# A two-layer image kernel: its last slots and last convolution as one written list, and the convolution's kernel from a stored fixed part

## The chip, the core and the metric

The kernel runs on one core of a Trainium2 chip. The metric is the device time of one execution in microseconds. Before the change the median of 3 runs is 1951.01 us (1948.79 to 1951.85).

## What is computed

Four images of 128 channels and 128x128 pixels go through two layers, each added to its input. Layer 0 works on pixels (tokens) of 128 channels; layer 1 is a 3x3 convolution with a gate per channel. `_gn` normalises groups of 4 channels over the whole image. Cut to what matters:

```python
def _block(t):                       # t: tokens x 128 channels
    t = _ln(t, ln0); y1 = _ln(t, ln1)
    t = t + silu(y1) @ W_out.T
    y2 = _ln(t, ln2); wht = y2 @ W_whiten.T
    k = square(relu(wht @ W_key.T))
    return t + sigmoid(wht @ W_recep.T) * (k @ W_value.T)
def _conv(x):                        # its weight is that of expert 0
    avg = x.mean(axis=(2, 3))
    se = sigmoid(relu(avg @ se_w1.T) @ se_w2.T)
    return (conv3x3(x, weight[0], padding=1) + bias[0]) * se[:, :, None, None]
x = x + _block(_gn(x)) + _block(_gn(x).transpose(0, 1, 3, 2)).transpose(0, 1, 3, 2)
x = x + _conv(_gn(x))
```

The two calls of `_block` see the same tokens in another order, so their sum is computed once and doubled.

## The kernel before, in words

**Layer 0** takes a pair of chunks of 512 pixels (a group g of `PAIR`) at a time: 16 groups an image, 64 in all. A group goes through some 40 named operations: `u` (normalise, ACT), `Tu` (turn, PE), `bn` (statistics, DVE), `nb` (norm terms, nine or six small operations on POOL, `norm_terms`), `t`, `g`, `b` (ACT, POOL, POOL), `z`, `Tz`, `silu`, `att`, `T`, then the third norm's terms, which are turned (`Tr`), copied (`rc`), stored to HBM (`W`, rd) and read back over all partitions (`R`), `cp` (y2), eight keys `pk`, their relu and square `re`, `sq` on ACT, eight values `kv`, the gate `pr`, `th`, `q`, and the sum into x (`S`, `x` on POOL), with the statistics `bx` for layer 1. The digits after a name are the half of the pair and the part.

**Layer 1** is a convolution on blocks of 16 rows (8 an image), computed in groups of four output rows by six transformed inputs: `p`, `q`, `p2`, `q2` and `v0` to `v5` on DVE, six products `c0` to `c5` on PE (three pairs of matmul passes each, `product`, lines 536 to 538), `e1`, `e3` on ACT, and `a`, `b`, `c`, `d`, `y0` to `y3`, `ca`, `d8` on DVE. The finished block is stored with one DMA of 1 MB (line 633). Each product takes one bank of PSUM; while layer 0 runs, all six share the one bank of tag `conv`.

**The order.** `ORDER` is written by hand: one slot runs each of its 114 operations with the group or block that is due (`u1:0` is for group s of slot s, `x11:3` for group s - 3). Inside `tc.manual_schedule()` each engine runs its instructions in the order written. The first 20 slots have an order of their own (`FIRST`). Slots go on to 68, so the last ones have ever fewer operations. The convolution of batch 3 stands behind the slots, outside the manual schedule, block after block.

**conv_setup(b)** (lines 253 to 330) makes the convolution's kernel of one image. It needs the statistics of the whole image: `mv` (line 226), `pm` (a matmul with `gmat`), mg, d, q, `pv`, ve, rs on POOL (line 240), avg, `p1`, a1, `p2`, the tanh `se` on ACT, `dg`, `pg`, `row`. Then cw, the 128x1152 weight, is scaled by rs and row (line 289), ident is added to its middle tap, and six transformed kernels uw0 to uw5 are formed from it (lines 305 to 328) on ACT and DVE. It is a generator: a slot gives it a step after every fifth operation, and what is left runs at the slot's end. It starts in the slot after the image's last group is done. The matmuls of the chain take banks of the tag `h`, which the keys use too (two banks). `input_norm(b)` is a similar, shorter chain for layer 0's input.

In the tables, PEld is the weight load, SP the queue that issues the DMAs.

Of the kernel before, what the change touches and what calls it, by code (L numbers as in the profile page):

```python
# [9 lines left out]
F32 = mybir.dt.float32  # L10
# [35 lines left out]
FIRST_SLOTS = 20  # L46
PAUSE = 2

SQUARES = ("AAAA", "AAAA")
FIRST_SQUARES = ("DAAA", "DAAA")  # L50

ON_GPSIMD = set()
ODD = {"v5a", "v5b", "c4", "c", "d", "y1", "y2", "ca", "d8", "c0", "y0", "c5", "y3"}
EVEN = {
    "p", "q", "v1", "v2", "p2", "q2", "c1", "e1", "c2", "a", "b", "v3", "v4", "c3", "e3",
# [5 lines left out]
def conv_preact_kernel(  # L61
# [63 lines left out]
    def bank(tag, name, bufs=2):  # L125
        return ps.tile([P, CH], F32, tag=tag, name=name, bufs=bufs)
# [93 lines left out]
    def col(name):  # L220
        return stat.tile([P, 1], F32, tag=name, name=name)
# [25 lines left out]
    def input_norm(b):  # L247
# [2 lines left out]
        nc.vector.scalar_tensor_tensor(nb, mg, -1.0, rs, ALU.mult, ALU.mult)  # L250
        gn0[b] = rs, nb

    def conv_setup(b):

        cw = wg.tile([P, 9, P], F32, tag="ring", name="cw", bufs=1)
        nc.sync.dma_start(cw, conv_w)
        d, mg, rs = yield from group_norm(st1.pop(b), "1")
        avg = col("avg")  # L260
        nc.vector.tensor_tensor(avg, d, rs, ALU.mult)
        mg6 = col("mg6")
        nc.vector.tensor_scalar(mg6, mg, 6.0, None, ALU.mult)
        yield
        p1 = bank("h", "p1")
        nc.tensor.matmul(p1[:NSE, 0:1], s1, avg, start=True, stop=True)
        yield
        a1 = stat.tile([NSE, 1], F32, tag="a1", name="a1")
        nc.vector.tensor_scalar(a1, p1[:NSE, 0:1], 0.0, None, ALU.max)
        yield  # L270
        p2 = bank("h", "p2")
        nc.tensor.matmul(p2[:, 0:1], s2, a1, start=True, stop=True)
        yield
        se = col("se")
        nc.scalar.activation(se, p2[:, 0:1], AF.Tanh, scale=0.5)
        yield
        nc.vector.tensor_scalar(se, se, 1.0, 0.5, ALU.add, ALU.mult)
        beta = col("beta")
        nc.vector.scalar_tensor_tensor(beta, se, cb, mg, ALU.mult, ALU.add)
        dg = wk.tile([P, P], F32, tag="u", name="dg")  # L280
        nc.vector.tensor_scalar(dg, ident, se, None, ALU.mult)
        yield
        pg = bank("h", "pg")
        nc.tensor.matmul(pg[:, :P], mean_of, dg, start=True, stop=True)
        yield
        row = wk.tile([P, P], F32, tag="u", name="row")
        nc.scalar.mul(row, pg[:, :P], float(C))
        yield
        nc.vector.scalar_tensor_tensor(
            cw, cw, rs, row.rearrange("p (o c) -> p o c", o=1).to_broadcast([P, 9, P]),  # L290
            ALU.mult, ALU.mult,
        )
        nc.vector.tensor_tensor(cw[:, 4], cw[:, 4], ident, ALU.add)
        yield
        w0, w1, w2 = (cw[:, 3 * a : 3 * a + 3].rearrange("p b c -> p (b c)") for a in range(3))
        uw, u = {}, {}

        def form(i, freed):
            while b > 0 and freed and (freed, b * NBLK - 1) not in multiplied:
                yield  # L300
            uw[i] = wg.tile([P, 3, P], F32, tag="uw", name=f"uw{i}", bufs=9)
            u[i] = uw[i].rearrange("p b c -> p (b c)")

        w6 = wk.tile([P, 3 * P], F32, tag="z", name="w6", bufs=2)
        nc.scalar.mul(w6, w1, 1.0 / 6)
        tmp = wk.tile([P, 3 * P], F32, tag="u", name="tmp")
        nc.vector.tensor_tensor(tmp, w0, w2, ALU.add)
        yield
        for i in (1, 2):
            yield from form(i, None)  # L310
        nc.vector.scalar_tensor_tensor(u[1], tmp, -1.0 / 6, w6, ALU.mult, ALU.subtract)
        nc.vector.scalar_tensor_tensor(u[2], tmp, -1.0 / 6, w6, ALU.mult, ALU.add)
        yield
        w4 = wk.tile([P, 3 * P], F32, tag="z", name="w4", bufs=2)
        nc.scalar.mul(w4, w0, 0.25)
        nc.scalar.mul(w6, w6, 0.5)
        nc.vector.tensor_tensor(tmp, w4, w2, ALU.add)
        yield
        yield from form(3, None)
        yield from form(4, 1)  # L320
        nc.vector.scalar_tensor_tensor(u[3], tmp, 1.0 / 6, w6, ALU.mult, ALU.add)
        nc.vector.scalar_tensor_tensor(u[4], tmp, 1.0 / 6, w6, ALU.mult, ALU.subtract)
        yield
        yield from form(0, 2)
        nc.scalar.copy(u[0], w4)
        yield
        yield from form(5, 3)
        nc.scalar.copy(u[5], w2)
        gn1[b] = mg, mg6, beta
        uws[b] = uw  # L330


    S = {}
# [196 lines left out]
    def wide(tag, name):  # L530
        return wg.tile([P, Q, W], F32, tag=tag, name=name)

    def product(i, k, v, tag="conv", bufs=1):
        pc = bank(tag, f"m{i}", bufs).rearrange("p (q w) -> p q w", w=W)
        u = uws[k // NBLK][i]
        nc.tensor.matmul(pc, u[:, 1], v, start=True, stop=False)  # L536
        nc.tensor.matmul(pc[:, :, 1:W], u[:, 0], v[:, :, 0 : W - 1], start=False, stop=False)  # L537
        nc.tensor.matmul(pc[:, :, 0 : W - 1], u[:, 2], v[:, :, 1:W], start=False, stop=True)  # L538
        return pc

    def conv_op(op, k, tag="conv", bufs=1):
        mg, mg6, beta = gn1[k // NBLK]
        first, last = k % NBLK == 0, k % NBLK == NBLK - 1
        d1, d2, d3, d4 = (rows(k, s) for s in range(4))
        eng = nc.gpsimd if op in ON_GPSIMD else nc.vector

        def put(name, tag):
            S[name, k] = t = wide(tag, name)
            return t

        def get(name):
# [8 lines left out]
        elif op == "q":  # L560
            stt(put("q", "vt"), d1, -4.0, d3)
        elif op == "v1":
            stt(put("v1", "v"), get("p"), mg6, get("q"), ALU.add)
        elif op == "v2":
            eng.tensor_tensor(put("v2", "v"), get("p"), get("q"), ALU.subtract)
        elif op == "p2":
# [7 lines left out]
        elif op == "v0a":  # L574
            v0 = put("v0", "v")
            eng.tensor_tensor(v0[:, 1:Q], d4[:, 0 : Q - 1], d2[:, 1:Q], ALU.subtract)
            if first:
                nc.vector.tensor_scalar(v0[:, 0:1], d2[:, 0:1], -1.0, mg, ALU.mult, ALU.add)
            else:
                eng.tensor_tensor(  # L580
                    v0[:, 0:1], S.pop(("edge", k - 1)), d2[:, 0:1], ALU.subtract
                )
        elif op == "v0b":
            stt(get("v0"), get("v0"), 4.0, get("p2"))
        elif op == "v5a":
            v5 = put("v5", "v")
            eng.tensor_tensor(v5[:, 0 : Q - 1], d1[:, 1:Q], d3[:, 0 : Q - 1], ALU.subtract)
            if last:
                nc.vector.tensor_scalar(
                    v5[:, Q - 1 : Q], d3[:, Q - 1 : Q], -1.0, mg, ALU.mult, ALU.add  # L590
                )
            else:
                eng.tensor_tensor(
                    v5[:, Q - 1 : Q], rows(k + 1, 0)[:, 0:1], d3[:, Q - 1 : Q], ALU.subtract
                )
                S["edge", k] = wg.tile([P, 1, W], F32, tag="edge", name="edge", bufs=2)
                eng.tensor_copy(S["edge", k], d4[:, Q - 1 : Q])
# [3 lines left out]
        elif op[0] == "c" and len(op) == 2 and op != "ca":  # L601
            i = int(op[1])
            multiplied.add((i, k))
            S["m", i, k] = product(i, k, S.pop((f"v{i}", k)), tag, bufs)
        elif op == "e1":
            nc.scalar.activation(put("e1", "yt"), S.pop(("m", 1, k)), AF.Identity, bias=beta)  # L606
        elif op == "e3":
            nc.scalar.copy(put("e3", "yt"), S.pop(("m", 3, k)))
        elif op == "a":
# [37 lines left out]
    def in_stats(g, h, src):  # L647
        b, p = g // NP, g % NP
        if b not in st0:
            st0[b] = stat.tile([P, NCH, 6], F32, tag="st0", name=f"st0_{b}")  # L650
        nc.vector.bn_stats(st0[b][:, p * PAIR + h, :], src)  # L651

    def layer0_op(op, g):
# [32 lines left out]


    def parsed(text):
        return [(w.split(":")[0], int(w.split(":")[1])) for w in text.split()]

    order, first = parsed(ORDER), parsed(FIRST)
    depth = max(k for op, k in order if op not in EVEN and op not in ODD)
# [26 lines left out]
    def slot(s, order, repeated):  # L719
# [12 lines left out]
        for n, (op, k) in enumerate(order):  # L732
            g = s - k
            if op in EVEN or op in ODD:
                c = g - NP - LAG
                if 0 <= c < (B - 1) * NP and (c % 2 == 1) == (op in ODD):
                    conv_op(op, c // 2)
            elif op in ("in0", "in1"):
                h = int(op[2])
                for i in now[:1]:  # L740
                    in_stats(i, h, S["in", i][:, ts(h, CH)])
            elif 0 <= g < B * NP and (op, g) not in issued:
                issued.add((op, g))
                layer0_op(op, g)
            if n % 5 == 4:
                for chain in chains:
                    next(chain, None)
        for chain in chains:
# [7 lines left out]
    with tc.manual_schedule():  # L756
        for s in range(FIRST_SLOTS):
            slot(s, first, False)
        phase["first"] = False
        for s in range(FIRST_SLOTS - PAUSE, slots):  # L760
            slot(s, order, s < FIRST_SLOTS)


    for k in range((B - 1) * NBLK, B * NBLK):
        for op in (
            "p q v1 v2 p2 q2 c1 e1 v3 v4 c2 a b v0a v0b c3 e3 v5a v5b c4 c d y1 y2 ca d8 "
            "c0 y0 c5 y3"
        ).split():
            conv_op(op, k, "h" if op in ("c1", "c3", "c0") else "tr", 2)


# [40 lines left out]
```

## Time and profile before

| what | value |
|---|---|
| median of 3 runs | 1951.01 us |
| the profiled execution, whole | 1947.18 us |
| its span in the profile | 1945.4 us |
| PE busy | 1825.0 us (94%) |
| DVE busy | 1351.5 us (69%) |
| ACT busy | 1278.1 us (66%) |
| POOL busy | 1147.5 us (59%) |
| granted TensorE clock, mean | 0.99 |
| DMA, mean | 67 GB/s |

The profile is one execution. Matmuls are pipelined and their ends are modelled, so a PE that is shown busy need not be at its peak; the distances between the starts of matmuls are firm. A wait is put down to the instruction that came last. "issue" is time in which the engine waited for nothing that the profile shows. PEclk is the granted share of the full TensorE clock. A row of a group or of the timeline gives start, duration, engine, line, operation, output<-inputs and shapes, and in brackets the idle time before it with who ended it.

### The profile page before, as it was taken

The numbers are of one execution on the slowest core, as the hardware profiler recorded it, in microseconds if no ns is written. First come the engines' busy times: TensorE is split into PE (matmuls) and PEld (weight loads), VectorE is DVE, ScalarE is ACT, GpSimd is POOL, SyncE is SP. The second block draws the span as 40 slices with busy tenths as digits, with TensorE's granted clock in tenths as the row PEclk, the third lists the DMA queues.
The fourth block names the chain that finished last, engine by engine and source line by source line (L and its number), as shares of the span: only waits on it lengthen the run. The fifth ranks groups of instructions, "written<-read, shape, count | busy, mean of one in ns | idle before, by whom it ended". The sixth has DMA issues, their size and how long they took to land.

```text
span 1945.4 us, 21642 instructions
## 1 busy us (share of the span) xinstructions
PE 1825.0 (94%) x6154; PEld 944.2 (49%) x6154; DVE 1351.5 (69%) x3309; ACT 1278.1 (66%) x2493; POOL 1147.5 (59%) x1939
## 2 busy tenths in 40 slices
PE   2399999999999999999999999999999999997998
PEld 1355555554545554554455455455455555543343
DVE  5466676665777776776677777667677666764997
ACT  0688998877677767676777677676676777752100
POOL 0877888774666766666766666666666667630000
PEclk9899999999999999999999999999999999999999
DMA  5211111120222221122232122112101111110111
GB/s 206 61 55 55 55 55 55 65 67 22 76 87 82 82 98 65 44 67 78 76 98 90 56 73 77 66 55 77 48 35 60 66 66 55 44 44 34 44 76 76
DMA packets 38567, 130.72 MB, mean 67 GB/s; under 512 B 5408, under 2 KB 7088, under 8 KB 30256
## 3 DMA queue, kind: packets, MB, share of 16 engines
q1 hardware_dynamic: 36160, 128.47, 19.1%
q10 hardware_dynamic: 2288, 0.87, 0.2%
q8 instruction: 49, 0.80, 0.2%
q14 instruction: 70, 0.57, 0.1%
HBM read 95.50 MB, written 33.82 MB: 66 GB/s over the span
## 4 chain that ended last, share of the span: by engine, by line
PE 75%; POOL 9%; DVE 6%; ACT 4%; issue 3%; DMA 2%; ACTq 0%; POOLq 0%; DVEq 0%
PE pk L471 19%; PE kv L498 18%; PE m L536 8%; PE m L537 8%; PE m L538 7%; PE pr L489 4%; PE att L433 4%; POOL rs L397 3%; DVE st L380 2%; PE tt L349 2%; PE ut L349 2%; ACT t L356 2%; PE z1t L349 2%; DVE st L651 1%; POOL rs L396 1%
## 5 line engine op out<-in xcount | busy, mean ns | idle before, releaser
L471 PE MATMUL pk<-y,wk_s 128*128 128x512 f32 x1024 | 503.0, 599 | 8.6 <-DVE h L485 4.4
L498 PE MATMUL kv<-h,wv 128*128 128x512 f32 x1024 | 483.7, 595 | 0.0
L475 ACT ACTIVATE h<-pk,kbias 128x512 f32<-128x512 f32 x512 | 350.9, 686 | 152.0 <-PE pk L471 150.6
L397 POOL TENSOR_TENSOR rs<-rs,nhalf 128x8 f32<-128x8 f32 x192 | 317.6, 1654 | 15.1
L498 PEld LDWEIGHTS kv<-h,wv 128*128 128x128 f32 x1024 | 187.8, 191 | 215.4 <-issue 185.1
L356 ACT ACTIVATE t<-ut,nb,rs 128x128 f32<-128x128 f32 x512 | 192.5, 464 | 146.7 <-POOL nb L403 146.7
L481 ACT ACTIVATE h<-h 128x512 f32<-128x512 f32 x479 | 282.8, 630 | 4.5
L471 PEld LDWEIGHTS pk<-y,wk_s 128*128 128x128 f32 x1024 | 182.9, 191 | 209.0 <-issue 149.9
L518 POOL TENSOR_TENSOR x<-x,r 128x512 f32<-128x512 f32 x128 | 163.5, 1277 | 185.5 <-DVE r L514 185.5
L380 DVE BATCH_NORM_STATS2 st<-t 128x6 f32<-128x128 f32 x1024 | 219.1, 276 | 22.5 <-POOL t L416 20.1
L356 ACT ACTIVATE z<-t,nb,rs 128x128 f32<-128x128 f32 x512 | 210.3, 488 | 21.9 <-POOL nb L403 21.9
L536 PE MATMUL m<-v,uw 128*128 128x512 f32 x384 | 201.6, 607 | 16.1 <-ACT e L606 6.5
L412 POOL TENSOR_TENSOR t<-t,g 128x512 f32<-128x512 f32 x128 | 162.9, 1280 | 73.3 <-ACT t L356 73.3
L537 PE MATMUL m<-v,uw 128*128 128x508 f32 x384 | 196.4, 593 | 0.0
L538 PE MATMUL m<-v,uw 128*128 128x508 f32 x384 | 195.6, 591 | 0.0
L392 POOL TENSOR_TENSOR rs<-st 128x8 f32<-128x8 f32 x192 | 56.5, 294 | 223.4 <-DVE st L380 207.9
L416 POOL TENSOR_TENSOR t<-t,b 128x512 f32<-128x512 f32 x128 | 162.4, 1275 | 6.9
L493 ACT ACTIVATE r<-pr,rbias 128x512 f32<-128x512 f32 x128 | 87.6, 684 | 90.2 <-PE pr L489 84.6
L433 PEld LDWEIGHTS att<-wo,y 128*128 128x128 f32 x1024 | 128.2, 193 | 21.6 <-issue 13.8
L433 PE MATMUL att<-wo,y 128*128 128x128 f32 x1024 | 136.8, 277 | 1.9 <-ACT y L427 1.5
L380 DVE BATCH_NORM_STATS2 st<-ut 128x6 f32<-128x128 f32 x512 | 111.6, 284 | 37.7 <-PE ut L349 37.7
L489 PE MATMUL pr<-y,wr_s 128*128 128x512 f32 x256 | 132.0, 597 | 5.0 <-ACT h L475 4.7
(125 smaller groups left out, 2427.7 us busy)
## 6 DMA issues: line engine op xcount, KB each, us to landing
x<-in_x SPq DMA_DIRECT2D x32, 1024.0 KB
R<-rd SPq DMA_DIRECT2D x128, 256.0 KB
out<-x SPq DMA_DIRECT2D x32, 1024.0 KB
xs<-in_x SPq DMA_DIRECT2D x48, 512.0 KB
cw<-in_conv_w SPq DMA_DIRECT2D x4, 576.0 KB
rd<-rrow SPq DMA_DIRECT2D x64, 4.0 KB
wv<-in_w_value_t ACTq DMA_DIRECT2D x1, 256.0 KB
wkt<-in_w_key_t ACTq DMA_DIRECT2D x1, 256.0 KB
```

The lines of the kernel that those rows point to most:

```text
L356: nc.scalar.activation(dst[:, s, :], src[:, s, :], AF.Identity, bias=nb[:, i : i + 1], scale=rs[:, i : i + 1],)
L380: nc.vector.bn_stats(st[:, h * SUB + s, :], src[:, s, :])
L397: gp.tensor_tensor(rs, rs, nhalf, ALU.pow)
L433: nc.tensor.matmul(att[:, ts(s, P)], y[:, ts(s, P)], wo, start=True, stop=True)
L471: nc.tensor.matmul(pk, wk_s[:, ts(j, P)], S["y2", g, h], start=True, stop=True)
L475: nc.scalar.activation(k, S["pk", g, h, j], AF.Relu, bias=kbias[:, j : j + 1])
L481: nc.scalar.activation(k, k, AF.Square)
L489: nc.tensor.matmul(pr, wr_s, S["y2", g, h], start=True, stop=True)
L498: nc.tensor.matmul(S["kv", g, h], wv[:, j, :], S.pop(("h", g, h, j)), start=(j == 0), stop=(j == NH - 1))
L536: nc.tensor.matmul(pc, u[:, 1], v, start=True, stop=False)
L537: nc.tensor.matmul(pc[:, :, 1:W], u[:, 0], v[:, :, 0 : W - 1], start=False, stop=False)
L538: nc.tensor.matmul(pc[:, :, 0 : W - 1], u[:, 2], v[:, :, 1:W], start=False, stop=True)
```

## The change

1. The slots run to 59 only. The last four groups of layer 0, the rest of batch 2's convolution, the chain of `conv_setup(3)` and the whole convolution of batch 3 stand in one list `END` inside the manual schedule. There, `u1:3` is for group 60 (63 - 3), a convolution operation's number counts blocks of batch 3 (negative ones are of batch 2), a `*` is one step of the chain, and `load` loads the last block.
2. In batch 3's convolution the six products take banks of five tags, `p2` and `q2` run on POOL, and the tiles of tag `v` are taken from the six buffers of tag `h`.
3. `conv_setup`: the six kernels are formed once, for batch 0, from the plain weight, and stored in HBM (`raw_u`). For each image they are fetched and then scaled by rs and row; to four of them ident is added with a factor. The row of gates comes from one matmul of the gate's hidden values over all columns with s2, instead of through `dg` and `pg`. A slot gives the chain a step after every third operation, not every fifth, and its steps are smaller.
4. `st0` has one buffer. ORDER and FIRST are as before.

```diff
+END_SLOTS = 4
+END = """
+    u1:3 Tu1:3 u0:3 d8:-5 z11:4 Tu0:3 bn00:3 Tz10:4 bn01:3 pk03:5 Tz11:4 silu0:4 x11:6
...
+    pk12:2 pk11:2 c:-3 x11:3 z10:0 S0:1 v5b:-3 sq10:2 Tz10:0 y2:-3 silu0:0 sq13:2 kv03:2
...
+    nb2:0 x10:2 re10:1 kv02:1 x11:2 Tr:0 kv03:1 c1:-2 th0:1 v3:-2 bx1:5 v5a:-2 q0:1 rc:0
...
+    d:-2 bx1:2 kv03:0 bx1:3 ca:-2 pk11:0 y1:-2 q0:0 re11:0 pr1:0 sq13:0 c0:-2 kv10:0 pk12:0
+    S0:0 th1:0 y0:-2 sq11:0 kv11:0 q2:-1 re12:0 d8:-2 sq12:0 c5:-2 kv12:0 p:-1 kv13:0 y3:-2
+    bx1:1 v1:-1 * c1:-1 q1:0 x10:0 x11:0 bx1:0 bx0:0 v3:-1 * e1:-1 v2:-1 v0a:-1 * * * c3:-1
+    * v4:-1 v0b:-1 * * p:0 e3:-1 * c2:-1 * v5a:-1 q:0 * v5b:-1 * * * a:-1 b:-1 v1:0 * * * *
+    c4:-1 * * * * p2:0 v2:0 q2:0 * p2:1 * c:-1 * * * * v3:0 v0a:0 * d:-1 y1:-1 c1:0 * * v4:0
+    c3:0 c0:-1 c4:0 d8:-1 v0b:0 y2:-1 ca:-1 y0:-1 c5:-1 p:1 v5a:0 * e3:0 y3:-1 q2:1 c:0 d:0
...
+    e3:7 c0:7 c5:7 c:7 d:7 y2:7 ca:7 y1:7 y0:7 d8:7 y3:7
+END_ON_GPSIMD = {"p2", "q2"}
...
+    raw_u = [dram.tile([P, 3, P], F32, tag=f"raw{i}", name=f"raw{i}", bufs=1) for i in range(6)]
     def conv_setup(b):
-        cw = wg.tile([P, 9, P], F32, tag="ring", name="cw", bufs=1)
-        nc.sync.dma_start(cw, conv_w)
...
+        def fetch(i):
+            tile_of(i)
+            nc.sync.dma_start(uw[i], raw_u[i])
+        if b == 0:
...
+            for i in range(6):
+                nc.sync.dma_start(raw_u[i], uw[i])
+        else:
+            for i in (1, 2, 3):
+                fetch(i)
+                yield
...
-        nc.tensor.matmul(pg[:, :P], mean_of, dg, start=True, stop=True)
+        a1 = stat.tile([NSE, P], F32, tag="a1", name="a1", bufs=1)
+        nc.vector.tensor_scalar(a1, p1[:NSE, 0:1].to_broadcast([NSE, P]), 0.0, None, ALU.max)
+        yield
+        pr = bank("h", "prow")
+        nc.tensor.matmul(pr[:, :P], a1, s2, start=True, stop=True)
...
+        def scale(i):
+            nc.vector.scalar_tensor_tensor(uw[i], uw[i], rs, over_taps, ALU.mult, ALU.mult)
+        def add_identity(i):
+            tap = {1: -1.0 / 6, 2: 1.0 / 6, 3: 1.0 / 12, 4: -1.0 / 12}[i]
...
+        scale(1)
+        yield
+        add_identity(1)
...
+            for i, freed in ((4, 1), (0, 2), (5, 3)):
+                while (freed, b * NBLK - 1) not in multiplied:
+                    yield
+                fetch(i)
...
+            where = ("kv", "tr", "tr", "ut", "ut", "conv")[i] if ending else "conv"
+            S["m", i, k] = product(i, k, S.pop((f"v{i}", k)), where)
...
-            if n % 5 == 4:
+            if n % 3 == 2:
...
-        for s in range(FIRST_SLOTS - PAUSE, slots):
+        for s in range(FIRST_SLOTS - PAUSE, B * NP - END_SLOTS):
             slot(s, order, s < FIRST_SLOTS)
-    for k in range((B - 1) * NBLK, B * NBLK):
-        for op in (
...
-            conv_op(op, k, "h" if op in ("c1", "c3", "c0") else "tr", 2)
+        chain = conv_setup(B - 1)
+        for op, n in parsed(END):
+            if op == "*":
+                next(chain, None)
+            elif op == "load":
+                load_block(len(blocks))
+            elif op in EVEN or op in ODD:
+                conv_op(op, (B - 1) * NBLK + n)
+            else:
+                layer0_op(op, B * NP - 1 - n)
```

## The prediction

> **What bounds the kernel now.** First the busy table of the page: PE 94% of the span, DVE 69%, ACT 66%, POOL 59%. So I looked for the stretches in which PE is not fed, with the busy times by stretch (columns: window, its length, busy us of PE, PEld, DVE, ACT, POOL with counts, then PEclk, DMA share, GB/s):
>
> ```profile
> 1606.00:1634.00 28.00, 28.00 (x98) 14.52 (x97) 19.23 (x46) 20.57 (x40) 19.63 (x35) 1.00 0.16 57
> 1634.00:1662.00 28.00, 27.79 (x96) 14.29 (x95) 18.74 (x50) 19.69 (x39) 17.18 (x27) 1.00 0.15 57
> ...
> 1746.00:1774.00 28.00, 28.00 (x69) 12.30 (x68) 14.86 (x28) 12.28 (x20) 2.54 (x2) 1.00 0.00 0
> 1774.00:1818.00 44.00, 28.87 (x61) 12.52 (x60) 27.35 (x56) 4.58 (x10) 1.82 (x2) 0.84 0.11 38
> 1818.00:1940.00 122.00, 121.72 (x286) 53.84 (x284) 107.84 (x193) 9.50 (x15) 0.00 (x0) 1.00 0.17 69
> 1940.00:1946.00 6.00, 0.00 (x0) 0.00 (x0) 0.45 (x1) 0.00 (x0) 0.00 (x0) 0.92 0.43 175
> ```
>
> The 28 us slots and the last convolution (1818 to 1940) are full. The hole is 1774 to 1818, with the clock at 0.84. The waits of PE there:
>
> ```profile
> PE m L536 <- DVE v L555: 4.7, 1, 4.7
> PE pm L229 <- DVE mv L226: 2.9, 1, 2.9
> PE m L536 <- DVE x L626: 2.9, 1, 2.9
> PE m L536 <- DVE v L565: 1.6, 1, 1.6
> PE pv L237 <- DVE q L234: 1.2, 1, 1.2
> PE p L266 <- DVE avg L261: 1.1, 1, 1.1
> ```
>
> This is batch 3's conv_setup: no product of the last convolution can start before the image's last group is normalised, and only the last products of batch 2 are left as cover. PE busy is modelled, so I count work by start-to-start distances: a 512-column matmul 0.857, a convolution product 2.562, four transposes 0.435, four att matmuls 0.89. The hole's 44 us hold 22.5 us of work: 21.5 are lost. Two products there ran slowly, from 1788.23 to 1792.46 and from 1805.81 to 1811.04, where 2.56 is usual; with 0.4 on the next one, 4.8 of the 21.5 are the clock.
>
> A smaller loss sits in the set-ups of batches 1 and 2. From one rd store to the next, plain slots take 29.1 and 26.9 in turn, but the two at 881.5 to 944.8 take 34.3 and 29.0: 7.3 us more for batch 1, and the same for batch 2. The waits of PE from 890 to 932:
>
> ```profile
> PE pr L489 <- ACT h L475: 1.5, 1, 1.5
> PE ut L349 <- ACT u L367: 1.3, 1, 1.3
> PE pk L471 <- DVE y L461: 0.8, 1, 0.8
> PE pv L237 <- DVE q L234: 0.4, 1, 0.4
> PE pk L471 <- ACT row L287: 0.4, 1, 0.4
> ```
>
> **The last slots and the last convolution as one list.** The list replaces slots 60 on. Both programs hold the same PE work from slot 60's first transpose: 116 transposes (12.6), 40 att matmuls (8.9), 107 of pk, kv and pr (91.7), 74 products (189.6), five rt and the chain (1.8), together 304.6 us. In the trace that stretch runs from 1611.41 to 1939.55, 328.1 us. So 23.5 are lost: 21.5 in the hole, 2.0 before it. After it come 5.9 us: y3 (0.69), and the store of the last block (1 MB at some 200 GB/s). The list also ends in c5, six DVE operations and y3, with c4 two products earlier (5.1 us against 4.4 of DVE work), so the tail stays.
>
> Walking along the list and adding PE work, the last kv13:0 ends at 165.0, c1:0 starts at 176.7, and 128.1 follow. Up to 165.0 the other engines' work is less (ACT some 114, DVE 110, POOL 89), and the groups' steps stand apart by about their durations: nb2:0 (3.1 us on POOL) has 2.6 us of PE work between bn21:0 and Tr:0, and R0:0 stands 6 us ahead of pk01:0 (the R issued at 771.78 was awaited until 775.16). The load of the last block is moved too: 3.4 us of PE work lie between it and its first reader u1:1, 7.4 to PE's own Tu1:1, against 5 for 1 MB. I take 2.5 us of waits for these 165 (the old slots lose 2.0 over the same work; bounds 1 and 9, as no trace shows these crossings).
>
> **The chain inside the list.** From kv13:0 at 165.0, with durations of the old chain:
> - q1 0.69, x11 1.27 on POOL, bx1 and bx0 1.3, v3 0.6, mv 1.02: mv ends at 170.2. PE has c1:-1 (to 167.6) and then pm waits 2.7. Queued behind pm is c3:-1.
> - pm to q: DVE also has v2, v0a, v4, v0b (2.7) between, q ends at 173.8; c3:-1 covers to 173.4, so pv waits 0.5. c2:-1 starts at 174.2, once e3 has emptied its bank.
> - ve, rs (0.56 on POOL), v5a, q, avg, v5b: p1 at about 176.9 behind c2:-1, a1, prow (0.3 of wait, 0.4 of work). a and b then empty c2's bank, c4:-1 starts at 178.5 (wait 0.6).
> - row (tanh 0.28, then 0.28), scale 0.55 (the shape of the 128x384 uw row) and add_identity 0.29 end at 180.2, under c4:-1, which ends at 181.1. c1:0 follows at once.
> The waits sum to about 5 (bounds 3 and 10). This is where most comes from: the path from mv to the first usable kernel was 1783.57 to 1806, 22 us; now it is about 11, and three products lie under it. c3:0 then waits for v3:0, behind three scales and adds on DVE: 0.6.
>
> A rule of the Trainium skill decides 2.6 of this. TensorE: Matmul & The Clock Gate, Part 1, says the array falls to half rate after an idle window of about 3.4 us. In the trace, PE was idle from 1775.86 to 1778.89 and the next product ran at full speed; only after the second such gap did the clock fall. My longest gap is 2.7 between whole products, so both give a warm c3:-1. Were the gap 1 us longer, the page's sum would add what the product at 1805.81 lost, 2.7; I keep that for the range.
>
> **p2 and q2 of the last convolution on POOL.** DVE drops two operations (1.2 us at their 0.6 spacing) from 13.6 us a block (107.84/122 of 15.37): 12.4, against 15.37 of PE. POOL pays 1.27 each (its row for 128x512). But SBUF — State Buffer, Who interferes with whom, speaks against it: a DVE instruction with two SBUF inputs and a GpSimd instruction that reads SBUF exclude each other, and the loser fully blocks. The trace agrees: under x on POOL (887.98, 1.27 us), p on DVE took twice its 0.68:
>
> ```profile
> 887.98 1.27 POOL L518 TENSOR_TENSOR x<-x,r 128x512 f32<-128x512 f32 x1
> 888.47 1.33 DVE L555 SCALAR_TENSOR_TENSOR p<-x 128x512 f32<-128x512 f32 x1
> ```
>
> With free engines DVE has 12.4 a block, with a full block 12.4 + 2.5 = 14.9, still under 15.37, but late for single products. I take 1 us for the eight blocks (bounds 0 and 4). The products' banks, now six tags, never bind: each is reused a block later.
>
> **The kernel's fixed part in HBM.** For batches 1 and 2, ACT loses five passes (2.5 us); DVE loses cw 1.41, 0.29, dg 0.28, tmp and uw 3.3, and gets six scales, four adds and row 4.8: about even. SP gets six fetches for one, some 0.35 us of issue each; they are issued well before use, and R and rd behind them have over 5 us. PE keeps five small matmuls. Steps come every 3 operations, not 5: pm now stands behind pr, so pr's 1.5 goes, but pk01 then needs pr's bank, which th0 empties about 1.2 later. ut's 1.3 goes with ACT's passes, the 0.8 on DVE stays. That is 1.5 a batch, 3 in all (bounds 8 gained, 1 lost). For batch 0, forming the fixed part comes ahead of mv: six DVE steps delay mv by 3.3, but pg, dg and the second half of p2's wait go; p2 stood at 436.56 and kv at 440.30, and I get kv at 440.2: nothing. The six stores stand on SP before rd and R of the next group, about 8 us late; their reader y at 449.85 has 16 us. Without that cover it would cost the difference. input_norm's closer steps: 0, within 1.
>
> **The sum.** 1611.4 - 3 + 176.7 + 2.5 + 5 + 128.1 + 0.6 + 1 + 5.8 = 1928.1 of span, 17.3 less than 1945.4. The profiled execution took 1947.18, 3.8 below the median of 1951.01; I take the difference from the median: 1933.7.
>
> **Rivals.**
> - The list is nearly free of waits and the set-ups gain their full bound: 1 + 3 + 0 instead of 2.5 + 5 + 1.6, and 8 in the middle: 10 us more, 1924. For it: ACT, DVE and POOL have a third of their time free in the list. Against: pm's wait is latency, which no order removes.
> - The waits move into the list: PE is in order and over 40 keys share two banks; each key waits for ACT, and ACT for the group's norm. At 9 + 10 + 4 us of waits the gain is 4, with the middle's 3 7: 1944. For it: Tr:0 and z10:0 to Tz10:0 have less cover than their length. Against: old slots with the same operations lose under 1%.
> - Slower: DVE becomes the bound of the last convolution by the shared port. Place: 1818 to 1940; price: eight times what DVE needs a block over 15.37. It decides from 15.37 + 17.3/8 = 17.5 a block; the full lock gives 14.9. Were each POOL operation to hold DVE for 3 us, a block would take 18.4: 1933.7 - 1 + 24 = 1957.
> - It does not do what it says: the cover was not short but the chain still ends later than c4:-1 (DVE far behind): the 21.5 stay, 1950. Against: DVE's own work between mv and add_identity is only 10 us.
>
> **How the numbers follow.** Forecast 0.62 (1928 to 1940), full gain 0.15, waits in the list 0.16, no gain 0.04, slower 0.03. What a measurement of this kernel can tell from no change is about 0.2%, 3.9 us. Below 1947.1 lie the first three less a little: faster 0.92, same 0.05, slower 0.03. The range from 1924 to 1945 leaves out the last two and the far ends of the second and third.
>
> **What would show it.** The hole before the first product of batch 3 with 5 us of waits, its longest at pm; kernel waits in the list under 3; clock 1.00 over the chain; 15.4 a block in the last convolution with p2, q2 near 1.3; rd to rd at batches 1 and 2 some 1.5 shorter. Wrong if z1t, rt or pk wait for more than 1 us at many places in the list, if the last convolution exceeds 125 us, or if half clock stands after pm.

## The result, and the profile after

The changed kernel takes 1943.56 us (median of 4 runs, 1942.53 to 1946.35), the kernel before beside it 1951.30. The ratio is 0.9965, interval 0.9948 to 0.9982: it is faster, by 7.7 us of the medians, where 17.3 were forecast. Its profiled execution took 1943.49, with a span of 1941.7. That one is at its median, while the profiled execution before was 3.8 under its own; so the spans differ by only 3.7. In what follows stretches of the traces are compared, not spans.

Two stretches tell the whole story. The first is the list, from the first transpose of slot 60 to the last product. Before it ran from 1611.41 to 1939.55, 328.1 us; after from 1623.17 to 1935.95, 312.8 us. The list gains 15.4 (forecast: 23.5 lost before, 9.1 after, so 14.4). PE's waits of after from 1590 to 1942:

```profile
PE m L663 <- DVE v L687: 2.1, 3, 1.2
PE pm L375 <- DVE mv L372: 1.9, 1, 1.9
PE m L663 <- DVE e L745: 0.7, 1, 0.7
PE att L560 <- DVE t L564: 0.6, 1, 0.6
PE m L663 <- ACT e L741: 0.5, 1, 0.5
PE prow L406 <- DVE a L403: 0.4, 1, 0.4
PE m L663 <- ACT e L739: 0.2, 1, 0.2
```

The columns after the colon are the sum, how often, and the longest. This stands against waits of 4.7, 2.9, 2.9, 1.6, 1.2 and 1.1 in the hole before; 6.4 us are left in the whole list.

The second stretch is everything ahead of it. The store of rd is one instruction a group, so it serves as a milestone (where a store is named by a slot, the number is that of its group). It stands later in after than in before by

| slot | 1 | 2 to 16 | 18 | 29 | 33 | 35 | 49 | 51 | 58 |
|---|---|---|---|---|---|---|---|---|---|
| us later | 1.5 | 2.2 | 6.5 | 6.9 | 6.9 | 10.0 | 10.3 | 11.7 | 11.8 |

The steps between 16 and 18, 33 and 35, 49 and 51 are the set-ups of batches 0, 1 and 2: they lose 4.4, 3.1 and 1.4, where I had 0, -1.5 and -1.5. The steps of input_norm lose 0.3 each. So 9.6 of the 15.4 were lost again before the list began, and 2.2 at the start, of which more below.

PE's waits of after around batch 1's set-up, 896 to 940:

```profile
PE pk L598 <- DVE y L588: 2.8, 1, 2.8
PE pm L375 <- DVE mv L372: 2.0, 1, 2.0
PE p L409 <- ACT row L412: 0.4, 1, 0.4
PE pk L598 <- ACT se L415: 0.3, 1, 0.3
```

pr's 1.5 and ut's 1.3 went, as the prediction said, but y's wait grew from 0.8 to 2.8, and pm, which had not waited, now waits 2.0 for mv. The sum is 5.5, against 4.6 before (the prediction's five lines and one more of 0.2): 0.9 more. That is not 3.1. The rest is in how the matmuls ran after the waits. The timeline of after (start, duration, engine, line, operation), first at batch 1, then at batch 2:

```profile
902.53 0.35 PE L375 MATMUL pm<-mv,gmat 128*128 128x1 f32 x2 [1.95 <-DVE mv L372]
902.74 1.95 PE L560 MATMUL att<-wo,y 128*128 128x128 f32 x8
904.49 1.91 PE L598 MATMUL pk<-y,wk_s 128*128 128x512 f32 x2
...
1364.28 0.35 PE L375 MATMUL pm<-mv,gmat 128*128 128x1 f32 x2 [1.96 <-DVE mv L372]
1364.50 1.14 PE L560 MATMUL att<-wo,y 128*128 128x128 f32 x8
1365.47 1.02 PE L598 MATMUL pk<-y,wk_s 128*128 128x512 f32 x2
```

These are the same instructions after the same wait. The next att and pk take 1.95 and 1.91 at batch 1, 1.14 and 1.02 at batch 2. In the rows by 0.2 us, PEclk is 0.50 from 902.86 to 906.27 and from 936.99 to 940.41 (batch 1, behind pm and behind pk), and from 1397.79 to 1401.21 (batch 2, behind pk only). Each stretch is 3.41 us long, PE works all through it, and so it costs half of that, 1.7. Between the stores that bound batch 1, PE idles 0.8 longer than before and its matmuls take 2.3 longer in sum; for batch 2 it is 0.8 and 0.6.

About half of what y's wait grew by is a collision. The rows of after ahead of y at batch 1 (the same two, 1.58 and 1.75, stand at batch 2):

```profile
933.11 1.58 POOL L645 TENSOR_TENSOR x<-x,r 128x512 f32<-128x512 f32 x1
933.48 1.75 DVE L687 SCALAR_TENSOR_TENSOR x<-e,e 128x512 f32<-128x512 f32 x1
935.69 0.68 DVE L588 TENSOR_TENSOR y<-tt,R 128x512 f32<-128x512 f32 x1
```

In before DVE's x<-e,e ran at 924.94, ahead of POOL's x at 926.20, and took 0.67. The added scales push it under POOL's x, and there it takes 1.1 more. The prediction counted such an exclusion for the last convolution alone.

Batch 0 is another case. The timeline of after, where its set-up forms the fixed part:

```profile
435.33 0.55 DVE L352 SCALAR_TENSOR_TENSOR u<-tmp,w 128x384 f32<-128x384 f32 x1
435.97 0.52 ACT L355 ACTIVATE w<-w 128x384 f32<-128x384 f32 x1 [5.27 <-DVE u L352]
...
436.80 0.68 ACT L620 ACTIVATE r<-pr,rbias 128x512 f32<-128x512 f32 x1
...
437.38 1.26 ACT L602 ACTIVATE h<-pk,kbias 128x512 f32<-128x512 f32 x2
...
438.75 0.56 PE L375 MATMUL pm<-mv,gmat 128*128 128x1 f32 x2 [4.90 <-ACT h L602]
```

ACT's halving of w6 (L355) waits 5.27 for DVE to have read w6. Behind it in ACT's order stand r and h, which empty the two banks of tag `h`, and pm needs one of them. mv itself, behind the forming on DVE, runs from 437.59 to 438.60, so both are late together. pm starts at 438.75 (2.1 of it is the slot's own shift), and half clock then lasts from 438.65 to 448.89, 10.2 us, against 6.8 before. In before the same matmul was

```profile
432.04 0.35 PE L229 MATMUL pm<-mv,gmat 128*128 128x1 f32 x2 [1.17 <-DVE mv L226]
```

**Theory.** The list gave its 15.4, and the changed set-ups cost 9.6: in batch 0 by forming ahead of mv, in batches 1 and 2 by mv's later place and the half clock behind the waits. **Rival:** the set-ups cost nothing, the shift of the milestones is chance of one profiled execution, and the list gives only the 7.7. A second rival for batches 1 and 2: the waits or the closer steps themselves are the loss, not the clock.

### The profile page after: what moved, and what is told of

Same layout as the page of the kernel before. It is cut to its first block, busy times and chain, and to the rows that moved or that the text cites. A ratio compares the mean times of both kernels' runs of the same rounds, so it can differ in the third digit from the quotient of the medians.

```text
span 1941.7 us, 21649 instructions
## 1 busy us (share of the span) xinstructions
PE 1825.3 (94%) x6154; PEld 946.6 (49%) x6154; DVE 1358.2 (70%) x3307; ACT 1271.6 (65%) x2477; POOL 1173.5 (60%) x1955
## 4 chain that ended last, share of the span: by engine, by line
PE 68%; POOL 14%; DVE 8%; ACT 4%; issue 3%; DMA 2%; ACTq 0%; POOLq 0%; SPq 0%; DVEq 0%
PE pk L598 17%; PE kv L625 16%; PE m L663 8%; PE m L665 7%; PE m L664 7%; POOL rs L524 5%; PE pr L616 4%; PE att L560 3%; DVE st L507 2%; PE tt L476 2%; PE ut L476 2%; ACT t L483 2%; PE z1t L476 1%; POOL t L543 1%; POOL x L645 1%
## 5 line engine op out<-in xcount | busy, mean ns | idle before, releaser
L663 PE MATMUL m<-v,u 128*128 128x512 f32 x384 | 198.9, 599 | 8.4 <-ACT e L739 4.7
L665 PE MATMUL m<-v,u 128*128 128x508 f32 x384 | 194.9, 589 | 0.0
L664 PE MATMUL m<-v,u 128*128 128x508 f32 x384 | 194.9, 589 | 0.0
```

## The experiments

Medians of the kernel before differed between the three sets of runs (1952.99, 1949.99, 1948.96), so ratios are compared across sets. "Slot 16" and "slot 58" are how much later that store of rd stands than in the first profile of before; "batch 0" to "batch 2" are the steps from 16 to 18, 33 to 35 and 49 to 51; "end" is the span's difference less that of slot 58, which is what the list or the last convolution gives.

| run | median us | ratio to before (interval) | slot 16 | batch 0 | batch 1 | batch 2 | slot 58 | end |
|---|---|---|---|---|---|---|---|---|
| the change | 1943.56 | 0.9965 (0.9948 to 0.9982) | 2.1 | +4.4 | +3.1 | +1.4 | 11.8 | -15.5 |
| e1_before_again | 1951.64 | 0.9996 (0.9987 to 1.0005) | 1.4 | -0.4 | 0.0 | 0.0 | 1.1 | +0.4 |
| e2_list_alone | 1936.73 | 0.9918 (0.9904 to 0.9932) | 4.4 | -0.3 | 0.0 | 0.0 | 4.0 | -15.0 |
| e3_setup_alone | 1956.10 | 1.0018 (1.0012 to 1.0025) | 0.3 | +5.7 | +1.4 | +1.4 | 9.5 | -2.2 |
| e4_formed_early | 1939.75 | 0.9933 (0.9918 to 0.9947) | 4.8 | -2.7 | +3.1 | +1.4 | 7.8 | -14.4 |
| e5_mv_first | 1938.33 | 0.9941 (0.9929 to 0.9954) | 3.7 | -0.8 | +3.0 | 0.0 | 6.4 | -14.3 |
| e7_coarse | 1934.65 | 0.9922 (0.9909 to 0.9934) | 1.1 | +0.3 | +0.7 | +0.7 | 3.7 | -13.7 |
| e6_coarse_carry | 1934.22 | 0.9917 (0.9904 to 0.9931) | 1.8 | +0.2 | +0.7 | +0.7 | 3.7 | -16.2 |
| e9_list_late | 1933.54 | 0.9916 (0.9903 to 0.9930) | 0.2 | -0.3 | +0.2 | 0.0 | 1.1 | -15.9 |
| e10_warm | 1942.20 | 0.9956 (0.9943 to 0.9968) | 1.7 | +7.4 | -0.2 | -0.2 | 9.1 | -14.0 |
| e11_list_warm | 1932.59 | 0.9911 (0.9898 to 0.9925) | 2.4 | -0.2 | 0.0 | 0.0 | 2.1 | -15.6 |
| e12_list_old_chain | 1940.96 | 0.9954 (0.9941 to 0.9968) | 3.7 | 0.0 | 0.0 | 0.0 | 3.4 | -8.5 |
| e8_p2q2_dve | 1942.95 | 0.9960 (0.9947 to 0.9974) | 1.2 | +5.8 | +1.4 | -0.3 | 8.3 | -11.6 |

### The kernel before once more (e1_before_again)

No edit.

> The kernel before, unchanged, profiled once more. Both theories: its time is 1951 within 3 us. It is here for the start: in the changed kernel the slots 2 to 16, ahead of any set-up, stood 2.2 us later than before. If that is chance of one execution, this profile's slots 2 to 16 differ from the first profile's by an amount of the same size, 1 to 3 us; if the first profile's start repeats within 0.5 us, the 2.2 belong to the change.

The same kernel's second profile stands 1.1 to 1.4 us later from the first slot on, and its span is 1946.8. So the start scatters by more than a microsecond without any change, and I put the 2.2 of after down to the start, not to the change. That is likely, not shown: e8 and e10, whose slots up to 16 are those of after, stand 1.2 and 1.7 later at slot 16, e3 0.3. The steps between slots repeat within 0.4.

### The list alone (e2_list_alone)

Batches 0 to 2 keep the old set-up and its pace; batch 3 takes the new one inside the list.

```diff
-            chains.append(conv_setup(b - 1))
+            chains.append(old_setup(b - 1))
...
-            if n % 3 == 2:
+            if n % 5 == 4:
...
+        if s == 0:
+            next(forming)
+        if s == 1:
+            chains.append(forming)
```

> The written list and its shorter chain, for the last batch only; batches 0 to 2 keep the old chain and its place at every fifth operation; the fixed part is formed and stored in slots 0 and 1. My theory: the list gives what its stretch of the trace shows, 15.4 us, and the changed set-ups cost 9 to 12 us ahead of it. Then this kernel takes 1951.3 - 15.4 = 1936, up to 1937.5 with what the forming adds in slots 0 and 1, and the stores of rd up to slot 58 stand within 1.5 us of the kernel before. Rival: the set-ups cost nothing, their shift is chance of one profiled execution, and the list gives only the 7.7 of the medians: 1943.5.

1936.73 was measured and 1936 to 1937.5 expected; the rival's 1943.5 is out. The steps of the three batches are back at 0 and the end gives 15.0. One miss: the stores up to slot 58 stand 4.0 behind, not 1.5. The forming costs about 3 at the very start, which e9 takes up.

### The set-up alone (e3_setup_alone)

The slots and the last convolution of before, all four batches with the new set-up at every third operation, `st0` with one buffer.

```diff
-            if n % 5 == 4:
+            if n % 3 == 2:
...
-        mg, mg6, beta = gn1[k // NBLK]
+        gn = gn1[k // NBLK]
```

> The slots and the last convolution of the kernel before, with the new set-up of all four batches at every third operation. My theory: the rd stores show + 4.4 behind batch 0, + 3.1 more behind batch 1, + 1.5 more behind batch 2, and 0.6 for the steps of input_norm, 9.6 in all by slot 58; the last batch's shorter chain gives some of the hole back, 3 to 10 us; the whole 1951 to 1958. Rival (the set-ups gain or are even): rd stores within 2 us at slot 58, and the whole 1941 to 1948.

It is slower than before, 1.0018, as expected: the set-ups lose 5.7, 1.4 and 1.4 (4.4, 3.1 and 1.5 expected). At the end the shorter chain gives only 2.2, less than the 3 to 10 expected (3.3 if it is counted from the last store of rd, as the expectation of e12 does). PE's waits of this run from 1590 to 1945 show where the rest of the hole went:

```profile
PE m L600 <- DVE v L620: 4.3, 1, 4.3
PE pm L312 <- DVE mv L309: 3.7, 1, 3.7
PE m L600 <- DVE x L691: 3.1, 2, 2.9
```

The kernel is ready sooner, but the last convolution still stands behind the chain, so its first product now waits just as long for its transformed input v, and pm waits even longer.

### The fixed part formed early (e4_formed_early)

The new set-ups stay; only the forming moves out of batch 0, which fetches as the others do.

```diff
-        if b == 0:
-            for a in ("w0", "w1", "w2"):
...
+        for i in (1, 2, 3):
+            fetch(i)
+            yield
```

> The changed kernel with the fixed part formed and stored in slots 0 and 1, so that batch 0's set-up fetches it as the others do. My theory: batch 0's loss of 4.4 comes from the forming ahead of mv and falls to that of batches 1 and 2 (1.5 to 3.1): 1943.6 less 1.3 to 2.9, 1941 to 1942.5. If forming was not what cost it (the closer steps alone), the loss behind batch 0 stays 4 to 5 and the time 1943.5.

1939.75: more gain than I expected. Batch 0 goes from 4.4 lost to 2.7 gained, 7.1 better, with one half-clock window of 3.41 instead of three in a row; about 2.7 is given back at the start. Batches 1 and 2 are as in the change. So in batch 0 it was the forming ahead of mv.

### mv ahead of the fetches (e5_mv_first)

```diff
-        for i in (1, 2, 3):
-            fetch(i)
-            yield
         mv = stat.tile([P, 2], F32, tag="mv1", name="mv")
...
+        if b < 3:
+            for i in (1, 2, 3):
+                fetch(i)
+                yield
```

> The kernel with the fixed part formed early (1939.8), with one order changed: for batches 0 to 2 the three fetch steps stand behind pm instead of ahead of mv. My theory: what batches 1 and 2 lose is mv's late place; with it earlier, pm's wait of 2.0 and the half clock behind it (about 1.7) go, while y's 2.8 stays: 2 to 3.7 less for each of the two batches, 1932 to 1936. Rival: the closer steps are the cause, and the wait moves to another matmul of the chain (pr's 1.5 or pv's): within 1.5 of 1939.8.

By its number the rival holds, just: 1938.33, 1.5 below 1939.75, and by the ratios (0.9941 and 0.9933) there is no gain. pm's wait went, and pr's 1.5 came back, as the rival said. Batch 2 lost nothing, batch 1 lost 3.0, and their waits are the same to 0.1 us (y 2.8, pr 1.5, 0.6, 0.4, 0.3). But in batch 1 half clock lasted from 930.69 to 937.52, in batch 2 there was none. So neither mv's place nor the waits explain the loss of a batch by themselves; the clock has to be counted.

### Few and large steps (e7_coarse, e6_coarse_carry)

mv first, fetches inside other steps, small steps joined, a step at every fifth operation; the fixed part formed in slot 4. In e6, what is left at a slot's end is carried over into the next.

```diff
-            chains.append(conv_setup(b - 1))
+            chains.append(coarse_setup(b - 1))
...
+            if chain in setting and chain not in late:
+                carried.append(chain)
+                continue
```

> The kernel with the fixed part formed early, with its loads in slot 3 and its steps in slot 4 instead of slots 0 and 1 (3 us less, if what they cost was the loads standing ahead of the first x loads), and for batches 0 to 2 a set-up with mv first, the fetches inside other steps, small steps joined, and a step every fifth operation as before the change. My theory (mv's place and the many close steps): batches 1 and 2 take no longer than in the kernel before, 34.3 and 29.0, or up to 1.5 less: 1939.8 - 3 - 4.5 = 1932, 1929 to 1933.5. Rival (fetches or the scales on DVE as such are the cost): 1935 to 1937.

> As the coarse set-up, with the steps that are left at the slot's end carried into the next slot, instead of being issued together at its end. My theory: y's wait of 2.8 comes from that heap, and goes: 1 to 3 us less for each of three batches, 3 to 8 below the coarse set-up without it. Rival: the first products of the batch then wait for their kernels, or the heap is hidden: within 1 us of it, or slower.

Both are at 1934 to 1935, where my theory had 1929 to 1933.5 and then 3 to 8 less. The half clock of batches 1 and 2 is gone (no row below 1.00 there), but pr's wait of 1.5 and y's of 1.6 stay, with another of 1.7 at the next y, and each batch loses 0.7. e7's 1934.65 lies between theory and rival (1935 to 1937). Carrying steps over changes nothing in the slots, so the heap at the slot's end was hidden, as e6's rival said: that part of my theory is wrong.

### Where the fixed part is formed (e9_list_late)

e2 with its loads in slot 3 and its steps in slot 4.

```diff
-        if s == 0:
+        if s == 3:
             next(forming)
-        if s == 1:
+        if s == 4:
             chains.append(forming)
```

> The list alone with the old set-ups (1936.7), with the fixed part's loads in slot 3 and its steps in slot 4. If the loads ahead of the first x loads cost the 3.0 us by which its slots stood behind: 1933.7, and slot 16's rd store within 0.7 of the kernel before. If forming costs its time wherever it stands: 1936.7.

1933.54, with slot 16 at 0.2: as expected. In e2 the three loads had stood on SP from 17.62 to 21.49, behind the first eight loads of x and ahead of those of xs; and the forming's steps ran on DVE from 56.46 to 62.58, among the statistics of the first groups. e9 moves both, so which of the two cost the 3 is not separated. By the ratios (0.9916 and 0.9918) the gain of 3 isn't resolved; by the milestones the four runs that load in slot 0 (e2, e4, e5, e12) stand 3.7 to 4.8 late and those that don't 0.2 to 2.4.

### Spare matmuls in the waits (e10_warm, e11_list_warm)

This separates wait from clock. Unused matmuls are put ahead of the waiting one, into the bank that it overwrites. They are extra work that the result has no use for.

```diff
         pm = bank("h", "pm")
+        if b < 3:
+            for _ in range(5 if b == 0 else 2):
+                nc.tensor.matmul(pm, wk_s[:, :P], wk_s, start=True, stop=True)
...
+        if (g, h, j) in ((34, 0, 0), (50, 0, 0)):
+            for _ in range(3):
+                nc.tensor.matmul(pk, wk_s[:, :P], wk_s, start=True, stop=True)
```

> The changed kernel with unused matmuls (0.86 us each, into the bank that the next matmul overwrites) in PE's queue where PE only waits: five ahead of pm in batch 0's set-up, two ahead of pm in batches 1 and 2, three ahead of the pk that waits for y in slots 34 and 50. They take no wait away. My theory: the loss of the set-ups is the half clock that follows a wait: after batch 0 some 5 us of 10.2 at half clock, 3.4 behind batch 1, 1.7 behind batch 2. Then the rd stores at slot 58 stand 2 to 4 behind the kernel before instead of 11.8, and the time is 1943.6 - 9 = 1934.5. Rival: the waits are the loss; then nothing is gained, or up to 2 us lost where a spare matmul ends later than the wait: 1943 to 1946.

For batches 1 and 2 this settles it. mv and y come when they came, PE is given 1.7 and 2.6 us more to do, PE stays at full clock, and the batches lose nothing: -0.2 each, where they lost 3.1 and 1.4. The timeline of e10_warm at batch 1:

```profile
903.35 1.98 PE L377 MATMUL pm<-wk_s 128*128 128x512 f32 x4 [0.28 <-ACT h L608]
905.17 0.28 PE L378 MATMUL pm<-mv,gmat 128*128 128x1 f32 x2
905.31 0.91 PE L563 MATMUL att<-wo,y 128*128 128x128 f32 x6
```

The six att passes after it now run at 0.15 each, where eight took 1.95. For batch 0 my expectation was wrong (7.4 lost instead of 4.4). PE's waits of e10_warm from 430 to 452 show why:

```profile
PE pm L377 <- ACT r L626: 3.7, 1, 3.7
PE p L403 <- issue: 1.1, 1, 1.1
```

The spare matmuls need the bank too, so they waited for ACT as pm had, and came on top. In the total little is left: batches 1 and 2 give 4.9, batch 0 takes 3.0, and the list, where the clock fell behind pm, gives 1.5 less than in after: 1942.2, not 1934.5.

In e11 the same is done to e9, one each ahead of pm and pv of batch 0, two ahead of pm in the list.

> The list alone with the late-formed fixed part (1933.5; 0.9916 of the kernel before), with unused matmuls where PE waits: one each ahead of pm and pv of batch 0's old set-up, two ahead of pm in the list. My theory: the half clock behind batch 0 (6.8 us of it in the kernel before, 3.4 lost) goes, and the one behind pm in the list where it fell (1.7): 1928.5 to 1930.5. Rival: within 1 us of 1933.5.

The rival holds: 0.9911 against 0.9916, no difference that can be told. In batch 0 the half clock fell from 6.8 to 3.4 us, and PE's idle time from 5.9 to 4.9, but the spare matmuls are 1.7 of work, and batch 0's step stayed (-0.2 against -0.3); and e9 had no half clock in the list to save. e11 is the fastest ratio of the study and e9 the simpler kernel; both beat the change.

### The list with the old chain (e12_list_old_chain)

```diff
-        chain = conv_setup(B - 1)
+        chain = old_setup(B - 1)
```

> The list alone (with the fixed part formed in slots 0 and 1, 1936.7), but the last batch too by the old chain, its steps at the list's places for a chain. It completes a square: the new chain without the list gave 3.3 us of the end. My theory: in the list the chain's length counts in full once the products under it are used up, since the first usable kernel then comes 8 to 11 us later: 1944 to 1948, so neither part gives much alone. Rival: the written order alone does it: 1937 to 1939.

In between: the end gives 8.5, against 15.0 in e2. With e3's 2.2 the square is complete: new chain alone 2.2, list alone 8.5, both 15 to 16. Each is worth more with the other. Of the 6.5 that the old chain costs in the list 1.7 is clock (two half-clock windows, 1788.39 to 1795.22, against e2's one) and 3.5 is waits (8.5 from 1780 on, 5.0 in e2). The rest I did not follow; in all it is less than the 8 to 11 I expected. PE in e12:

```profile
1804.05 1.13 PE L758 MATMUL m<-v,uw 128*128 128x512 f32 x2 [0.58 <-DVE uw L535]
...
1808.80 1.13 PE L758 MATMUL m<-v,uw 128*128 128x512 f32 x2 [1.93 <-DVE v L782]
```

The first usable kernel is late by 0.58 only: even the old chain nearly fits under the products that the list keeps for it. What it pays are many small waits: 1.35 more at pv, 0.9 at pg where prow waits 0.4, 0.8 more at v.

### p2 and q2 back on DVE (e8_p2q2_dve)

```diff
-END_ON_GPSIMD = {"p2", "q2"}
+END_ON_GPSIMD = set()
```

> The changed kernel with p2 and q2 of the last convolution back on DVE. By the prediction they are worth nothing while DVE has 12.4 to 13.6 us of work for a block of 15.4, and on POOL they cost 0 to 4 us by the shared port, taken as 1: so 1942.5 to 1944, and 128 us from c1:0 to the last product in both. If DVE's time was short in the list, 1945 or more.

The time is the same (0.9960 and 0.9965, 1942.95). In the trace, from c1:0 to the last product's last pass it is 128.7 in after and 131.1 here. All 2.4 lie in the second product of batch 3:

```profile
1808.99 1.78 PE L663 MATMUL m<-v,u 128*128 128x512 f32 x2 [1.90 <-DVE v L687]
1810.57 1.90 PE L664 MATMUL m<-v,u 128*128 128x508 f32 x2
```

v comes 0.7 later (1.9 for 1.16), and behind this wait the clock fell, 1.7. From there on both take 122.1. So p2 and q2 on POOL gain 0.7 at one place where DVE is behind, and nothing in the blocks.

This run differs from after in batch 3 alone, so its first three set-ups are a second execution of the same instructions. At batch 2 PE waits for mv and y as in after, but the clock stays at 1.00, and the step is -0.3 where after has +1.4:

```profile
1362.58 0.35 PE L375 MATMUL pm<-mv,gmat 128*128 128x1 f32 x2 [1.96 <-DVE mv L372]
1394.80 1.13 PE L598 MATMUL pk<-y,wk_s 128*128 128x512 f32 x2 [2.81 <-DVE y L588]
```

## Why the prediction was right and where it failed

- **What bounds the kernel, and the list: right.** The stretch gave 15.4, where 14.4 was forecast. The last kv of the list ends 166.9 after its start (167.5 with my 2.5 of waits), and from there c1:0 follows after 16.3 (forecast 16.1, with 5 of waits). The longest wait is pm's, 1.9 where I had 2.7; the wait for v3:0 is 1.16 where I had 0.6. After 1812 there is no wait of PE at all: the port's 1 us was nothing.
- **The step that failed: "The kernel's fixed part in HBM"**, with its "1.5 a batch, 3 in all (bounds 8 gained, 1 lost)" and, for batch 0, "I get kv at 440.2: nothing". Measured: 4.4, 3.1 and 1.4 lost, 8.9 in all, 0.6 more with input_norm. Two terms of it failed.
  - For **batch 0** I counted six DVE steps ahead of mv and 3.3 us. They took 4.7 (432.88 to 437.59), the first two 1.0 and 1.43 beside POOL's g, where the others take 0.55. And I did not follow ACT's queue: w6's halving waits there for DVE, and behind it stand the two operations that free pm's bank. pm was 6.7 later and kv after the chain 5.3, of which 2.1 is the shift of the whole slot. Of the 4.4, 3.4 is idle time of PE between the two stores (9.3 against 5.9) and 1.0 is slower matmuls, with half clock one window longer. e4 shows the cause by taking the forming away.
  - For **batches 1 and 2** I took away the waits that the new order removes and added none. Three fetch steps ahead of it put mv behind bn, bx0 and v1 on DVE: pm waits 2.0, and y, behind scales, adds and the collision with POOL, 2.0 more. These waits by themselves cost nothing in sum: in e8's batch 2, with the same waits at full clock, PE idles 0.8 longer than in before, but its matmuls take 1.1 less (why was not looked into), and the step is -0.3. So the term was -0.3 a batch, not -1.5. The loss is a cost that the step put at nothing: half clock after a wait, two windows in batch 1 and one in batch 2.
- **The clock rule was read too simply.** The prediction took from the Trainium skill (TensorE: Matmul & The Clock Gate, Part 1) an idle window of about 3.4 us, and so held gaps up to 2.7 to be free. The same part says that the window is free-running, 4096 cycles or 3413 ns. The traces agree with that: every half-clock stretch that the end of the trace doesn't cut lasts one or more times 3.413 us, and in after they start at 438.65, 902.86, 936.99 and 1397.79, which are 136.00, 10.00 and 135.00 times 3.4133 apart. What decides is how much of one such window PE idles, and the grid lies anew in each execution. pm's 1.95 at batch 1 fell into one window; at batch 2 the grid cut it, at 1363.66, into 1.33 and 0.62, and the clock stayed. That was the difference in the two stretches shown above.
- **The size follows.** Over the change, e3, e4, e5, e8 and e10, the steps of batches 1 and 2 with no half-clock window are at -0.3 to 0.0, those with one at 1.4, those with two at 3.0 to 3.1. The times say the same of the whole: e9, with the list and the old set-ups, is at 0.9916 and the change at 0.9965, 9.6 us apart with intervals that do not meet, where the milestones gave 9.6 for the set-ups and some 2 for the start. In the list it was chance in the forecast's favour: pm's wait of 1.9 left the clock at 1.00 in after, e6 and e9, but it fell there in e2, e4, e5, e7, e8 and e10, and their ends are worth 0.5 to 4 less.
- **The rivals.** "The waits move into the list" gave 1944, close to the measured time, but that is luck twice over. The list did not have these waits; and its sum is off: 23.5 less the 23 of waits is a gain of 0.5, not 4, and with the middle's 3 the rival stands at 1947.5. None of the four said that the set-ups would take it back.
- **What stays open:** the 2.2 at the start of after (1.4 of it can be chance, by e1); whether e9's 3 us over e2 are in the times, not only in the traces; and where before spends 3 to 4 us in most of its executions, as its two profiles, 1947.18 and 1948.58, lie that much under the medians of 1951.01 and 1951.64.

## What to carry to other kernels

When a step moves, follow each of its instructions down its own engine's queue, and ask who stands behind it: not only what waits, but what frees a bank. Give every new wait of PE of some 1.5 us or more a second price, the 1.7 us of a half-clock window times the chance that the wait lies in one window. And where a gain needs two things at once, here an order that keeps work for the gap and a chain that fits into it, test them apart before shipping a third that only looked free.

## What the runs showed of the hardware

- A wait of 2 us can cost nothing or 1.7 us more, by the phase of a window that runs on its own. Over 14 traces, from 400 us to the last products, with the grid taken from each trace's half-clock stretches: of 168 full-clock windows with 0.8 to 1.55 us of idle PE, 1 was followed by half clock; of 32 with 1.55 to 1.95, 14; of 25 above 1.95, 24. (Idle PE is the time between the end of one matmul and the start of the next; the ends are modelled.) So about half a window of idle PE decides, less than the whole window that I had assumed.
- Once the clock is half, less idling keeps it there: all half-clock windows with under 0.1 us idle were followed by full speed, but of 19 with 0.1 to 1.25 us idle 14 were followed by another at half (before at 436.33, with 1.13).
- Matmuls whose result nobody reads were enough to hold the clock in e10's batches 1 and 2 (no half clock, -0.2 each). In its batch 0 they needed what pm waited for, and cost 3.0.
